# Turning the weights of GRU layers 1 to 3 in three places of two half-steps each, with the input weights and W in one PSUM bank

## The chip, the cores and the metric

The kernel runs on one core of a Trainium2 chip. The metric is the device time of one execution in microseconds (us). A run is a median of several executions. Of the engines, PE is TensorE (PEld its weight load), ACT is ScalarE, DVE is VectorE, POOL is GpSimd, and SP is SyncE, which here only issues DMAs.

## The reference, cut to what matters

```python
# layer 0: a gated graph network, 16 graphs of N = 1024 nodes, C = 128 features, L = 4 GRU layers
h = relu(layernorm(x))
for i in range(L):
    hw = h @ weight[i]
    m = adj.T @ hw                      # per graph
    gx = m @ w_ih[i].T + b_ih[i]        # 128 -> 3 x 128
    gh = h @ w_hh[i].T + b_hh[i]
    r, z = sigmoid(xr + hr), sigmoid(xz + hz)
    n = tanh(xn + r * hn)
    h = (1 - z) * n + z * h
x = x + h * mask
# layer 1: four graph convolutions with batch norm
h = relu(layernorm(x))
for i in range(4):
    h = batch_norm(relu(adj @ (h @ W[i]) + b[i]))
out = x + h
```

The change concerns only the weights of the GRU layers. The products with `weight[i]` and `w_ih[i]` follow each other without anything in between but the aggregation over nodes, so the kernel joins them: `weight[i] @ w_ih[i].T` is computed once per layer (`w_mT` in the code), and the aggregation works on `h` itself. For that the input weights, the hidden weights and `weight[i]` ("W" below, `w_g` in the code) have to be turned (transposed) once per layer, by PE.

## The kernel before

One program, `exact_path`, does the work; `general_path` (lines 20 to 356) is a fallback that is entered only when the inputs fail a test at run time. Features lie on the partitions, and a graph's 1024 nodes lie on the free axis in two halves of 512. The adjacency of a graph is held as eight rows of 128x1024, rounded to fp32r; the features are split into a high and a low part (`ghw`, two tiles), so the aggregation `aggregate_rows` (L521 to L531) is 32 matmuls of 128x512: eight rows, two parts, two halves. They add up in two PSUM banks, `pm`, which ACT copies to `m` (L944).

Two streams, `sa` and `sb`, each carry one graph at a time through its four layers. `half_step(one, two)` (L1035) aggregates one stream's layer while the gates of the other run: it splits `one`'s features (`split_step`, by eight turns `hw_g` at L498 in the first half-steps), does the gate products of `two` for its first and second half of nodes (`gate_step`, L955; six products each at L972, then sigmoid, tanh and sigmoid on ACT at L984, L990, L991, and the combination on DVE at L985, L986 and L997 to L999), then the first half of `one`'s aggregation, `agg_step(0)`, then whatever was passed as `halfway`, then `agg_step(1)`. What was passed as `gated` comes between the second gates and the aggregation. The kernel's clock counts half-steps and starts at 3; the stage before it, written out by hand from L1122, carries both graphs through their first aggregation. Half-step 3 is `half_step(sa, sb)`, with the aggregation of `sa` for its layer 1 and the gates of `sb` for its layer 0; half-step 4 is `half_step(sb, sa)`, and so on, two half-steps for each layer.

The order of instructions on an engine is the order of the code in the part under `manual_schedule(engines=every)`, which before ends with half-step 4. In the rest of the gated network it is the order of the code for PE, POOL and SP, and a scheduler orders ACT and DVE.

The weights come in natural layout by DMA on SP (`load_layer`, L457; layer 0 at the start, layers 1 to 3 later, then `w_g` for layers 1 to 3 at L1183). They are turned by `turn_layer` (L466): three turns of the hidden weights into one PSUM bank (L470) and an ACT copy of 384 columns (L471), three turns of the input weights into another (L474) and a copy (L477), one turn of W into a third (L479) and a copy of 128 columns (L481). `join_layer` (L484) multiplies the two turned matrices (L487) and copies the product to `w_mT` (L488). All these PSUM tiles come from `tmp`, a pool of two banks used in turn, which also serves `hw_g` and, in the part before half-step 5, `g_r` of the second half.

Layer 0 is turned and joined at the start, between L1129 and L1132. Layer 1 is turned at the half-way point of half-step 3 and joined at its end, layer 2 likewise in half-step 4, and layer 3 is turned and joined at once after that. The calls are:

```python
half_step(sa, sb, looks, lambda: turn_layer(prep, w_g, 1))
join_layer(1)
half_step(sb, sa, None, lambda: turn_layer(prep, w_g, 2))
join_layer(2)
turn_layer(prep, w_g, 3)
join_layer(3)
```

The hidden state of later half-steps leaves by DMA and comes back turned: DVE transposes blocks (L711), SP stores and reloads (L591, L598), ACT and DVE split it (L905, L906). SP also issues transposing loads of the adjacency (L610), from tiles that POOL casts (L609), and the rows of later graphs (L573), which POOL rounds (L578); a small POOL copy, `pace` (L1054), ties its queue to the gates. While the first graphs are read, DVE looks over each row (`first_look`, L604).

Of the kernel before, what the change touches and what calls it, by code (L numbers as in the profile page):

```python
# [8 lines left out]
F32 = mybir.dt.float32  # L9
# [7 lines left out]
P = 128  # L17
# [324 lines left out]
def exact_path(  # L342
# [21 lines left out]
    nc = tc.nc  # L364
    B, N, C = x.shape
    L = g_weight.shape[0]
    NB = N // P
# [11 lines left out]
    def acc(tag, name):  # L379
        return ps_m.tile([P, HALF], F32, tag=tag, name=name)  # L380

    def tmp(name):
        return ps_t.tile([P, HALF], F32, tag="tmp", name=name)
# [5 lines left out]
    def flat(name):  # L389
        return keep.tile([P, NB, C], F32, tag="x", name=name, bufs=4)  # L390
# [14 lines left out]
    ident = const.tile([P, P], F32, tag="ident", name="ident")  # L405
# [57 lines left out]

    turned = {}

    def turn_layer(prep, w_g, i):  # L466

        pt = tmp(f"pt_whh{i}")
        for g in range(3):
            nc.tensor.transpose(pt[:, g * P : (g + 1) * P], wns["hh", i][:, g, :], ident)  # L470
        nc.scalar.copy(w_hhT[:, i, :], pt[:, : 3 * P])  # L471
        pt = tmp(f"pt_wih{i}")
        for g in range(3):
            nc.tensor.transpose(pt[:, g * P : (g + 1) * P], wns["ih", i][:, g, :], ident)  # L474

        w_ihT = prep.tile([P, 3 * C], F32, tag="w_ihT", name=f"w_ihT{i}", bufs=1)
        nc.scalar.copy(w_ihT, pt[:, : 3 * P])  # L477
        pg = tmp(f"pt_g{i}")
        nc.tensor.transpose(pg[:, :P], w_g[:, i, :], ident)  # L479
        w_gT = prep.tile([P, P], F32, tag="w_gT", name=f"w_gT{i}", bufs=1)  # L480
        nc.scalar.copy(w_gT, pg[:, :P])  # L481
        turned[i] = w_gT, w_ihT

    def join_layer(i):  # L484
        w_gT, w_ihT = turned[i]
        pw = tmp(f"pt_wm{i}")
        nc.tensor.matmul(pw[:, : 3 * P], w_gT, w_ihT, start=True, stop=True)  # L487
        nc.scalar.copy(w_mT[:, i, :], pw[:, : 3 * P])  # L488
# [45 lines left out]
    with ExitStack() as st:  # L534
# [32 lines left out]
        def first_look(b, j, ts):  # L567
            for k, t in enumerate(ts):
                look(b, t, j, k)
# [42 lines left out]
        def transposes(batches):  # L612

            for b, rows in batches:
                adjT = turned_tile(f"adjT{b}")
                ahead = transpose_rows(b, rows[0], 0, adjT)
                for j in range(NB):
                    go = ahead
                    if j + 1 < NB:
                        ahead = transpose_rows(b, rows[j + 1], j + 1, adjT)  # L620
                    go()
                    yield j
                nc.gpsimd.dma_start(adjT_d[b].rearrange("k p n -> p k n"), adjT)
                yield NB
# [136 lines left out]
        def behind(*inss):  # L761

            es = ExitStack()
            for ins in () if written[0] else inss:
                es.enter_context(tc.issue_after(ins.ins))
            return es
# [264 lines left out]
        def due(place):  # L1031
            for go in agenda.pop((clock[0], place), ()):
                go()

        def half_step(one, two, gated=None, halfway=None):  # L1035

            feed.next_step()
            one.split = []
            if one.i == 0:
                two.fetch()  # L1040
            due("ins")
            if one is sb and one.i == 0 or written[0] and one is sa:
                feed.jobs = transposes([(s.b, s.rows) for s in (sa, sb)])
            if one.i > 0:
                one.split_step()
                two.fetch()
                feed.some(2)
            two.gate_step(0)
            two.half_away(0)
            two.first_four()  # L1050
            if feed.full or (clock[0], "mid") in agenda:

                pace = small.tile([P, 1], F32, tag="pace", name=f"pace{clock[0]}")
                nc.gpsimd.tensor_copy(pace, two.new[:, :1])  # L1054
                feed.store()
                due("mid")
            due("outs")
            one.split_back(0, two.last_act, two.mid_dve)
            one.split_back(1, two.last_act, two.mid_dve)
            if one.i > 0:  # L1060
                feed.some(1)
            two.gate_step(1, None, one.split)
            two.half_away(1)
            with behind(two.first_act):
                due("late")
            if one.i == 0:
                feed.some(1)
            two.last_four()
            if gated:
                gated()  # L1070
            if one.i == 0:
                with behind(two.last_m):
                    one.split_step()
            one.agg_step(0)
            if halfway:
                halfway()
            with behind(two.last_act, two.last_dve, *one.split):
                due("gap")
            feed.some(NB if written[0] and one is sa else 1)
            one.agg_step(1)  # L1080
            two.finish()
            clock[0] += 1

        sa, sb = Stream(0), Stream(1)
        every = {getattr(mybir.EngineType, e) for e in ("PE", "DVE", "Activation", "Pool", "SP")}
        with tc.tile_pool(name="prep", bufs=1) as prep, tc.manual_schedule(engines=every):


            pt = tmp("pt_idle")
# [14 lines left out]
            w_g = flat("w_g")[:, :L, :]  # L1104
# [21 lines left out]
            sa.sums(range(4, 5))  # L1126
            norm_invert(sa.norm, 0, BH)
            sa.centred(range(4))
            turn_layer(prep, w_g, 0)  # L1129
            sa.centred_high(0)  # L1130
            sa.sums(range(5, 7))
            join_layer(0)  # L1132
            pt = tmp("pt_idle1")
# [51 lines left out]
            sb.agg_rows(range(4))  # L1185
            turn(sb.y, "in1", h1)
            sb.hT = h1
            sb.agg_rows(range(4, NB))

            def looks():  # L1190
                for j in range(4, NB):
                    first_look(1, j, raw1[j])

            sa.plan(0)
            sb.plan(1)
            half_step(sa, sb, looks, lambda: turn_layer(prep, w_g, 1))
            join_layer(1)
            half_step(sb, sa, None, lambda: turn_layer(prep, w_g, 2))
            join_layer(2)
            turn_layer(prep, w_g, 3)  # L1200
            join_layer(3)
        with tc.manual_schedule(engines={getattr(mybir.EngineType, e) for e in ("PE", "Pool", "SP")}):
            written[0] = False
            for s in range(2, B // 2 * L):
                half_step(sa, sb)
                half_step(sb, sa)
            assert not agenda, sorted(agenda)
            sb.gate_step(0)
            sb.gate_step(1)
            with tc.issue_after(sb.last_act.ins):  # L1210
                sa.rest()
            sb.finish()
# [5 lines left out]
    pt = tmp("pt_flag")  # L1218
# [212 lines left out]
    pt = tmp("pt_idle_end")  # L1431
# [4 lines left out]
    for b in range(B):  # L1436
# [3 lines left out]
        for n0, n in pieces(b):  # L1440
# [5 lines left out]
            tag = turns[count % len(turns)]  # L1446
            count += 1
            pt = (tmp(f"pt_o{b}_{n0}") if tag == "tmp" else acc(tag, f"pt_o{b}_{n0}"))[:, :n]
# [8 lines left out]
@with_exitstack  # L1457
def kernel(ctx: ExitStack, tc: tile.TileContext, *args):
    nc = tc.nc
    flagp = ctx.enter_context(tc.tile_pool(name="flagp", bufs=1))  # L1460
    flag_i = flagp.tile([1, 1], I32, tag="flag", name="flag_i")
    exact_path(tc, flag_i, *args)
    inexact = nc.values_load(flag_i, min_val=0, max_val=1 << 24)  # L1463
    with tc.If(inexact > 0):
        general_path(tc, *args)
# [41 lines left out]
```

## Time and profile before

| what | value |
|---|---|
| median of three runs | 1796.03 us (1793.29 to 1797.85) |
| profiled execution, from first to last instruction (its span; no other time is given for it) | 1795.0 us |
| mean granted TensorE clock | 0.997 |
| PE busy in the span | 1763.4 us |
| DVE, ACT, POOL busy | 1258.8, 1107.2, 389.4 us |
| PE idle for ACT `ghw` (L905), whole span | 11.1 us, 7 times |
| turns of hidden weights, input weights, W (L470, L474, L479): first and last start | 6.7 to 82.6 us |
| products (L487): first and last start | 8.6 to 83.9 us |

A row of a timeline gives the start from the span's beginning, the busy time of the merged instructions, the engine, the source line, the operation, the tiles (written <- read), the shape and the count; brackets hold the engine's idle time ahead of the row and who ended it. PE is pipelined and a row's end is modelled: rows overlap, so the work of one step is better read from its start to the next one's start. An fp32 matmul shows as two rows (x2), an fp32r matmul and a 128-column turn as one. Line numbers are those of the kernel before; after the change most lines are one lower in the helpers and higher towards the end.

### The profile page before, as it was taken

To read this page: it belongs to the slowest core of one execution; us is meant where nothing else is said; L and a number is where in the kernel's file an instruction comes from. 1 tells how busy PE (TensorE), PEld (TensorE's weight loads), DVE (VectorE), ACT (ScalarE), POOL (GpSimd) and SP (SyncE) were. 2 spreads that over 40 slices of the span, in tenths; PEclk is the share of its full clock that TensorE was granted. 3 is DMA by queue.
4 is the path that set the end of the run, shared out by engine and by line. 5 is a ranking of instruction groups with operands and counts; after the bars stand their busy time and mean duration, and the time that the engine had idled before them with its cause. 6 is when DMAs were issued, how large, how long until landed. Compare 5 with 4: busy or idle time off the path is not lost. (4 is left out here: it accounts for less than half of the span.)

```text
span 1795.0 us, 22286 instructions
## 1 busy us (share of the span) xinstructions
PE 1763.4 (98%) x6742; PEld 1194.0 (67%) x6742; DVE 1258.8 (70%) x2308; ACT 1107.2 (62%) x1717; POOL 389.4 (22%) x417
## 2 busy tenths in 40 slices
PE   9999999999999999999999999999999999999997
PEld 6555565556565556556556555677778888888886
DVE  7567867867776776777786776676666666666665
ACT  5346456556556555755655655477777767768765
POOL 4213322332332331422342333110100000000011
PEclk9999999999999999999999999999999999999999
DMA  7448676776676766766767667778866566767667
GB/s 253 112 125 268 171 223 237 200 207 225 205 211 211 236 191 193 263 197 168 263 185 209 241 194 209 268 277 299 284 223 244 209 244 215 246 223 240 241 220 263
DMA packets 363968, 399.11 MB, mean 222 GB/s; under 512 B 159820, under 2 KB 240496, under 8 KB 363840
## 3 DMA queue, kind: packets, MB, share of 16 engines
q1 hardware_dynamic: 343088, 322.54, 57.1%
q0 software_dynamic: 20224, 74.80, 11.5%
q8 instruction: 55, 0.90, 0.2%
q14 instruction: 73, 0.60, 0.1%
q10 hardware_dynamic: 528, 0.26, 0.0%
HBM read 266.95 MB, written 96.99 MB: 203 GB/s over the span
## 5 line engine op out<-in xcount | busy, mean ns | idle before, releaser
L525 PE MATMUL pm<-row,ghw 128*128 128x512 f32 x2048 | 505.6, 403 | 11.8 <-ACT ghw L905 11.1
L525 PEld LDWEIGHTS pm<-row,ghw 128*128 128x128 f32 x2048 | 384.3, 189 | 124.5 <-issue 26.5
L525 PE MATMUL pc_m<-wide,chw 128*128 128x512 f32 x1024 | 246.1, 396 | 0.0
L609 POOL CAST half<-row 128x1024 bf16<-128x1024 f32 x128 | 148.8, 1171 | 327.2 <-DMA adjT<-half 312.5
L525 PEld LDWEIGHTS pc_m<-wide,chw 128*128 128x128 f32 x1024 | 190.5, 188 | 42.3 <-issue 4.3
L991 ACT ACTIVATE z<-g_z,brz 128x512 f32<-128x512 f32 x128 | 87.5, 684 | 171.3 <-PE g_z L972 171.2
L525 PE MATMUL pc_g_r<-wide,chw 128*128 128x512 f32 x464 | 187.0, 403 | 0.3 <-ACT chw L502 0.3
L578 POOL CAST row<-stage 128x1024 fp32r<-128x1024 f32 x112 | 131.5, 1181 | 243.6 <-DMA stage<-in_adj_dram 221.1
L525 PE MATMUL pc_g_z<-wide,chw 128*128 128x512 f32 x464 | 181.0, 390 | 0.0
L985 DVE SCALAR_TENSOR_TENSOR r<-g_hn,vecs,r 128x512 f32<-128x512 f32 x128 | 95.0, 742 | 118.3 <-ACT r L984 76.6
L1237 DVE CAST wide<-block 128x1024 fp32r<-128x1024 bf16 x160 | 109.8, 692 | 73.2 <-PE pc_m L525 46.2
L1237 DVE CAST wide<-packed 128x1024 fp32r<-128x1024 bf16 x160 | 110.2, 691 | 72.1 <-PE pc_g_z L525 53.9
L944 ACT COPY m<-pm 128x512 f32<-128x512 f32 x128 | 68.5, 586 | 147.9 <-PE pm L525 147.9
L990 ACT ACTIVATE r<-r,vecs 128x512 f32<-128x512 f32 x128 | 91.8, 717 | 104.0 <-DVE r L986 104.0
L997 DVE TENSOR_TENSOR h<-h,r 128x512 f32<-128x512 f32 x96 | 81.8, 852 | 101.6 <-ACT r L990 101.6
L1235 ACT CAST wide<-packed 128x1024 fp32r<-128x1024 bf16 x96 | 100.6, 1048 | 59.1 <-PE pc_m L525 28.3
L972 PE MATMUL g_r<-m,w_mT 128*128 128x512 f32 x256 | 131.5, 595 | 2.8 <-ACT m L944 2.3
L1235 ACT CAST wide<-block 128x1024 fp32r<-128x1024 bf16 x96 | 100.6, 1049 | 52.3 <-PE pc_g_z L525 27.7
L972 PE MATMUL g_xn<-m,w_mT 128*128 128x512 f32 x256 | 130.7, 592 | 0.0
L972 PE MATMUL g_z<-m,w_mT 128*128 128x512 f32 x256 | 130.7, 592 | 0.0
L998 DVE TENSOR_TENSOR h<-h,z 128x512 f32<-128x512 f32 x128 | 118.7, 931 | 4.8 <-ACT z L991 1.9
L1285 DVE BATCH_NORM_STATS2 stats<-feat 128x6 f32<-128x512 f32 x128 | 84.1, 686 | 47.0 <-ACT feat L1284 45.9
(187 smaller groups left out, 2804.3 us busy)
## 6 DMA issues: line engine op xcount, KB each, us to landing
block<-adjT_d SPq DMA_DIRECT2D x256, 256.0 KB, 4.7
packed<-adjT_d SPq DMA_DIRECT2D x256, 256.0 KB, 5.5
stage<-in_adj_dram SPq DMA_DIRECT2D x120, 512.0 KB, 4.8
adjT_d<-adjT POOLq DMA_DIRECT2D x16, 2048.0 KB, 8.3
cross_h<-t_h SPq DMA_DIRECT2D x90, 256.0 KB, 3.2
n_h<-cross_h SPq DMA_DIRECT2D x360, 64.0 KB, 2.0
xmid_d<-x POOLq DMA_DIRECT2D x16, 512.0 KB, 5.4
y<-ymid_d POOLq DMA_DIRECT2D x16, 512.0 KB, 5.9
```

The source lines that it names most:

```text
L525: nc.tensor.matmul(pm[hf], hw[s][:, j * P : (j + 1) * P], rows[j][:, hf * HALF : (hf + 1) * HALF], start=(j == 0 and s == 0), stop=(j == N ...
L578: nc.gpsimd.tensor_copy(t, stage[j % 4])
L609: nc.gpsimd.tensor_copy(t, row.bitcast(F32))
L972: nc.tensor.matmul(po, wT[:, i, g * C : (g + 1) * C], rhs, start=start, stop=stop)
L985: nc.vector.scalar_tensor_tensor(r, phn, b_hn(i), r, ALU.add, ALU.mult)
L990: nc.scalar.activation(r, r, AF.Tanh, bias=b_in(i))
L991: self.last_act = nc.scalar.activation(z, pz, AF.Sigmoid, bias=brz[:, 3 * i + 1 : 3 * i + 2])
L997: nc.vector.tensor_sub(ho, hin, r)
L998: nc.vector.tensor_mul(ho, ho, z)
L1235: nc.scalar.copy(r, t)
L1237: nc.vector.tensor_copy(r, t)
L1285: nc.vector.bn_stats(stats[:, b * NH + hf, :], dst)
```

## The change

`turn_layer` is cut in two. `turn_hh(i)` turns and copies the hidden weights. `turn_ih(prep, w_g, i)` turns the input weights and W into the four quarters of one bank, and empties it by one copy of 512 columns into one tile, `w_both`, of which the product takes its two operands. The pool `prep` stays open longer.

Of layers 1 to 3, the hidden weights are turned at the half-way point of the half-step ahead (layer 1: between the sixth and the seventh row of `sb`'s first aggregation), the input weights and W after the gates of the layer's own half-step, and the product is made at its half-way point, followed there by the next layer's hidden weights. Layer 3 moves from the end of half-step 4 into half-step 5, which stands in the part that a scheduler orders for ACT and DVE. For layer 0 both functions are called where `turn_layer` was.

```diff
-    def turn_layer(prep, w_g, i):
+    def turn_hh(i):
         pt = tmp(f"pt_whh{i}")
         for g in range(3):
             nc.tensor.transpose(pt[:, g * P : (g + 1) * P], wns["hh", i][:, g, :], ident)
         nc.scalar.copy(w_hhT[:, i, :], pt[:, : 3 * P])
+
+    def turn_ih(prep, w_g, i):
         pt = tmp(f"pt_wih{i}")
         for g in range(3):
             nc.tensor.transpose(pt[:, g * P : (g + 1) * P], wns["ih", i][:, g, :], ident)
-        w_ihT = prep.tile([P, 3 * C], F32, tag="w_ihT", name=f"w_ihT{i}", bufs=1)
-        nc.scalar.copy(w_ihT, pt[:, : 3 * P])
-        pg = tmp(f"pt_g{i}")
-        nc.tensor.transpose(pg[:, :P], w_g[:, i, :], ident)
-        w_gT = prep.tile([P, P], F32, tag="w_gT", name=f"w_gT{i}", bufs=1)
-        nc.scalar.copy(w_gT, pg[:, :P])
-        turned[i] = w_gT, w_ihT
+        nc.tensor.transpose(pt[:, 3 * P :], w_g[:, i, :], ident)
+        both = prep.tile([P, 4 * C], F32, tag="w_both", name=f"w_both{i}", bufs=1)
+        nc.scalar.copy(both, pt)
+        turned[i] = both[:, 3 * C :], both[:, : 3 * C]
...
-            turn_layer(prep, w_g, 0)
+            turn_hh(0)
+            turn_ih(prep, w_g, 0)
...
-            sb.agg_rows(range(4, NB))
+            sb.agg_rows(range(4, 6))
+            turn_hh(1)
+            sb.agg_rows(range(6, NB))
             def looks():
+                turn_ih(prep, w_g, 1)
                 for j in range(4, NB):
                     first_look(1, j, raw1[j])
+            def ahead(i):
+                join_layer(i)
+                if i + 1 < L:
+                    turn_hh(i + 1)
             sa.plan(0)
             sb.plan(1)
-            half_step(sa, sb, looks, lambda: turn_layer(prep, w_g, 1))
-            join_layer(1)
-            half_step(sb, sa, None, lambda: turn_layer(prep, w_g, 2))
-            join_layer(2)
-            turn_layer(prep, w_g, 3)
-            join_layer(3)
+            half_step(sa, sb, looks, lambda: ahead(1))
+            half_step(sb, sa, lambda: turn_ih(prep, w_g, 2), lambda: ahead(2))
         with tc.manual_schedule(engines={getattr(mybir.EngineType, e) for e in ("PE", "Pool", "SP")}):
             written[0] = False
-            for s in range(2, B // 2 * L):
+            half_step(sa, sb, lambda: turn_ih(prep, w_g, 3), lambda: ahead(3))
+            half_step(sb, sa)
+            for s in range(3, B // 2 * L):
```

More of the change, by code (lines that the diff above doesn't have):

```diff
@@ L1085, in exact_path @@
         every = {getattr(mybir.EngineType, e) for e in ("PE", "DVE", "Activation", "Pool", "SP")}
-        with tc.tile_pool(name="prep", bufs=1) as prep, tc.manual_schedule(engines=every):
+        prep = st.enter_context(tc.tile_pool(name="prep", bufs=1))
+        with tc.manual_schedule(engines=every):
             pt = tmp("pt_idle")
```

## The prediction

> **What bounds the kernel now.** I read the head of the page first, then the waits of TensorE (PE), then the stretch that the edit touches, row by row. From the page (busy time with its share, then the PE and clock rows of the forty slices):
>
> ```profile
> span 1795.0 us, 22286 instructions
> PE 1763.4 (98%) x6742; PEld 1194.0 (67%) x6742; DVE 1258.8 (70%) x2308; ACT 1107.2 (62%) x1717; POOL 389.4 (22%) x417
> ...
> PE   9999999999999999999999999999999999999997
> ...
> PEclk9999999999999999999999999999999999999999
> ```
>
> PE is busy in every slice at full clock. A busy PE is not yet a PE at its peak, but the 31.6 us it sat idle are the only time that can be won without removing matmuls. Where they lie in the first 110 us is told by PE's waits in that window (waiter, then releaser: total us, times, longest):
>
> ```profile
> PE pt_wm L487 <- ACT w_gT L481: 1.0, 2, 0.6
> PE pt_g L479 <- ACT w_hhT L471: 0.7, 3, 0.2
> ...
> PE pt_wih L474 <- ACT w_mT L488: 0.3, 1, 0.3
> PE hw_g L498 <- ACT w_mT L488: 0.2, 1, 0.2
> PE g_r L972 <- DVE ghw L503: 0.2, 1, 0.2
> ```
>
> Four of these five are the weight turning: PE waits for a ScalarE (ACT) copy of what it has just turned. The timeline of PE shows the largest such place, the end of half-step 4 (start us, busy us, instruction; in brackets the idle time ahead of it):
>
> ```profile
> 75.80 0.49 PE L470 MATMUL pt_whh<-ident,wn_hh 128*128 128x128 f32 x3
> 76.13 0.49 PE L474 MATMUL pt_wih<-ident,wn_ih 128*128 128x128 f32 x3
> 76.86 0.33 PE L479 MATMUL pt_g<-ident,w_g 128*128 128x128 f32 x1 [0.24 <-ACT w_hhT L471]
> 76.94 3.91 PE L525 MATMUL pm<-row,ghw 128*128 128x512 f32 x16
> 80.69 0.81 PE L487 MATMUL pt_wm<-w_ihT,w_gT 128*128 128x384 f32 x2
> 81.33 0.49 PE L470 MATMUL pt_whh<-ident,wn_hh 128*128 128x128 f32 x3
> 82.17 0.55 PE L474 MATMUL pt_wih<-ident,wn_ih 128*128 128x128 f32 x3 [0.35 <-ACT w_mT L488]
> 82.56 0.33 PE L479 MATMUL pt_g<-ident,w_g 128*128 128x128 f32 x1
> 83.51 0.91 PE L487 MATMUL pt_wm<-w_ihT,w_gT 128*128 128x384 f32 x2 [0.62 <-ACT w_gT L481]
> 84.26 1.39 PE L498 MATMUL hw_g<-ident,h 128*128 128x128 f32 x8
> 85.48 1.02 PE L972 MATMUL g_r<-h,w_hhT 128*128 128x512 f32 x2
> ```
>
> From 80.69 to 85.48 no aggregation matmul stands between a turn and the step that needs its copy. Rows overlap, since ends are modelled, so I count from start to start below.
>
> **What the Trainium skill says.** "PSUM — Partial Sum Buffer", section on bank collisions: guard PSUM by bank and quadrant, not by address. So a turn into a bank waits for the copy out of it; the trace agrees (L479 waits 0.24 us for the copy of L471, its bank's last reader). "Perfetto Trace Analysis", Matmuls: independent groups should rotate through banks so that a copy overlaps the next group. Here two banks carry three turns and a product, and the 82.17 row shows the rotation running dry. "ScalarE: Activation LUTs", What ACT_TABLE_LOAD costs: an activation with immediate operands takes 186 ns plus 0.833 ns per element, and successive ones overlap by about 93 ns. The trace has 478 ns for 384 columns and 266 ns for 128, somewhat less than the 506 and 293 of that rule, with starts about 0.1 us before the previous end. I use the trace's durations.
>
> **The change part by part.** Unit prices, start to start: three turns 0.32 us (54.99 to 55.31), so 0.107 each; the product L487 0.64 (59.88 to 60.52); eight unhindered hw_g turns 0.88 (39.67 to 40.55); one gate product 0.86; sixteen aggregation matmuls 3.75 (56.13 to 59.88). The number of turns and products is the same before and after, so what can change is stall.
>
> *Stalls removed.* Half-step 3: 55.31 to 56.05 is 0.74, less 0.32 of work, 0.42 of stall; hw_g 60.52 to 61.36 is 0.84, less 0.43, 0.41. Half-step 4: 76.13 to 76.86 stalls 0.41; 81.33 to 82.17 stalls 0.52; 82.56 to 83.51 stalls 0.95 - 0.11 = 0.84; 83.51 to 84.26 stalls 0.11; hw_g, 84.26 to 85.48, is 1.22 against 0.88, 0.34. Sum 0.83 + 2.22 = 3.05 us. Check by whole steps: from the last gate product to the next gate, half-steps 3 and 4 take 11.38 (50.47 to 61.85) and 14.18 (71.30 to 85.48); half-step 5, without turns, takes 8.15 (94.93 to 103.08), with hw_g 9.03. The excess is 2.35 + 5.15 = 7.50; 21 turns and 3 products are 2.25 + 1.92 = 4.17; 3.33 is stall. So 3.05 can be named and 0.28 can't.
>
> *Hidden weights of layer 1, moved ahead.* turn_hh(1) puts 0.32 us of PE work at about 38 us, between rows 4-5 and 6-7. Soon after, g_r waits for VectorE (DVE): 44.84 to 46.08 is 1.24 against 0.86, a stall of 0.38, and DVE is busy with its looks without a gap from 38.3 to 46.5, independent of PE. So the 0.32 moves into a stall: a further gain of 0.32. Without that cover it is 0. Its copy falls into ACT's 2.77 us wait ahead of the m copies at 39.64. Its data were asked for at 26.30 and land in about 3.3 us.
>
> *Input weights and W, after the second gate.* Four turns (0.43) now stand ahead of the first aggregation row, into one bank, emptied by one 512-column copy. The nearest row is the m copy of 128x512, 586 ns. That copy is behind tanh and the z sigmoid on ACT's queue. In half-step 3 z runs 53.20 to 53.87, so the copy ends at about 54.4. PE turns at 51.33 to 51.76, aggregates 3.75, and asks for it at 55.5: cover 1.1 us. In half-steps 4 and 5 the same sum gives 76.4 against 74.2 and 100.0 against 97.2: cover 2.2 and 2.8. If the cover failed, each microsecond of lateness would be a microsecond of PE. w_g was asked for at 43.53 and lands in 3.7 to 5.1, at the latest 48.6, against 51.3.
>
> *Product and next hidden weights at half way.* The two tmp banks have been emptied by then: product and turn go through without waiting, their copies (about 0.5 each) have the second 3.75 us of aggregation as cover, and hw_g at its end finds both banks free.
>
> *Layer 3 a half-step later.* Layer 3 is now joined in the middle of half-step 5; its first gate is three half-steps on, in half-step 8. So nothing waits for it.
>
> *Layer 0.* One copy (0.59) in place of two (0.49 and 0.27, overlapping): L487 could start at about 8.54 instead of 8.63. Four aggregation matmuls later PE waits for POOL's row anyway (10.02 to 11.46 is 1.44, of which 0.94 work). Worth 0.
>
> *Queues.* DVE, POOL and SP keep their order. The two built programs differ in one wait that matters: the load of wn_hh2 now waits for turn_hh(1) on PE, whose buffer it evidently takes, where it waited for DVE until 41.34. PE is there at 38.4, so SP isn't held; the next load waits for DVE as before.
>
> *New borders.* Turns stand between aggregation rows in four new places. In 30.64 to 40.55, 9.91, I find 8.15 + 0.88 for step and hw_g and 0.88 for eight turns in the middle, 0.11 each: borders cost nothing there. Not shown is a border with a semaphore on PE's queue; I bound it between 0 and 0.15 us each and take 0. It can't gain, as it adds a wait.
>
> *Sum.* 3.05 + 0.32 = 3.4 us, with ends 3.65 (the unnamed 0.28 goes too) and 2.5 (borders 0.6, turn_hh(1) uncovered 0.3). Nothing later should give it back: the transpose loads on SP end at 86.97, and SP then waits 6.8 us for DVE before its next store at 93.82; after that, stores, reloads and stage loads are all paced by the gates, and PE's largest later wait, 11.1 us in all for ghw of L905, starts from the gates as well. Span 1795.0 - 3.4 = 1791.6. The page gives no other time of its execution; the median of the runs shown, 1796.0, is 1.0 above its span, so I forecast 1792.6.
>
> **Rivals.**
> - *The gain is swallowed.* PE starts half-step 5 earlier, but a chain with its own clock (transpose loads, POOL casts, staging of the next batch) doesn't, and a later wait absorbs the lead. For: POOL waits 312.5 us in all for transpose loads. Against: the 6.8 us of slack just named, and no PE wait for POOL rows after 13 us. Leaves 0 to 1 us: 1795.5.
> - *More than the stalls.* The waits for L905 differ between batches (1.28 at five places, 1.93 and 2.80 at two). They hang on how DMA traffic falls. Another phase could bring the two to 1.28, another 2.2 us: 1790.4.
> - *Slower: the reload falls behind the transposes.* With PE ahead by 3.4, the SP queue could have a transpose load in front of the hidden-state stores L591 at each half-batch. Seven L905 waits going from 1.3 to the 2.8 seen once cost 10 us, less 3.4: 1802.6. It decides once the lead exceeds the 6.8 us of slack, or if loads are stretched by as much. Only the 2.80 speaks for it.
> - *It doesn't do what it says:* w_both's copy is late in half-step 3. It would take a lateness of over 1.1 us; gain then 2.4 or less, inside the range.
>
> **How the numbers follow.** Forecast 0.62, its own range 1791.4 to 1794.5; swallowed 0.16; more 0.15; slower 0.07. Three runs of the kernel before span 4.6 us, so a median may be off by some 1.5 either way. Low end 1789.0 (the larger gain less that), high end 1797.0 (swallowed plus that). About 0.3%, 5.4 us, is what a measurement of this kernel can tell from no change. Faster by that needs the larger gain with noise on its side: 0.15. Slower by that is only the third rival: 0.06. Same: 0.79.
>
> **What would show it.** Right: no PE idle at the product or the turns between 50 and 100 us; half-step 3 from 11.4 to about 10.4, half-step 4 from 14.2 to about 10.4, half-step 5 from 8.15 to about 9.2; the first gate of half-step 6, at 103.08, about 3.4 earlier, and that lead kept at 1700. Wrong: a wait of the product for w_both; a lead of 3.4 at 100 us that is gone by 350; L905 waits above 1.3 in number; or g_r at about 46 us later than before.

## The result, and the profile after

Sixteen runs of each kernel, taken in turns, give a median of 1792.83 us (1790.73 to 1796.87) for the changed kernel against 1796.66 us (1793.29 to 1799.67) for the one before. The ratio is 0.9981 with a 95% interval of 0.9974 to 0.9989: 2.0 to 4.7 us faster, and less than the 0.3% that was called no change.

The head of the changed kernel's page:

```profile
span 1789.3 us, 22282 instructions
PE 1759.7 (98%) x6742; PEld 1191.5 (67%) x6742; DVE 1264.2 (71%) x2308; ACT 1107.8 (62%) x1713; POOL 388.9 (22%) x417
```

The number of PE instructions is unchanged, and ACT has lost the four W copies. The span is 5.7 us below the other profile's 1795.0, more than the medians differ, so a single pair of spans must not be read as the gain. It is read from the half-steps. First PE's waits in the first 110 us of the changed kernel:

```profile
PE pt_idle L1093 <- POOL ident masks.py:199: 2.4, 1, 2.4
PE pt_wm L486 <- ACT w_both L480: 0.7, 1, 0.7
PE g_z L971 <- ACT z L990: 0.6, 1, 0.6
PE g_r L971 <- DVE ghw L502: 0.3, 1, 0.3
```

Of the four kinds of waits for weights that stood in the list of before, one is left, and its one case is layer 0's product at 7.6 us. The timeline of PE through half-step 4, the stretch that was shown of before:

```profile
69.63 1.02 PE L971 MATMUL g_z<-m,w_mT 128*128 128x512 f32 x2
70.49 0.49 PE L477 MATMUL pt_wih<-ident,wn_ih 128*128 128x128 f32 x3
70.82 0.27 PE L478 MATMUL pt_wih<-ident,w_g 128*128 128x128 f32 x1
70.85 3.94 PE L524 MATMUL pm<-row,ghw 128*128 128x512 f32 x16
74.62 0.81 PE L486 MATMUL pt_wm<-w_both 128*128 128x384 f32 x2
75.27 0.49 PE L470 MATMUL pt_whh<-ident,wn_hh 128*128 128x128 f32 x3
75.51 3.92 PE L524 MATMUL pm<-row,ghw 128*128 128x512 f32 x16
79.27 1.03 PE L497 MATMUL hw_g<-ident,h 128*128 128x128 f32 x8
80.14 1.02 PE L971 MATMUL g_r<-h,w_hhT 128*128 128x512 f32 x2
```

No row has a bracket: PE goes from turns to aggregation to product to turns without a wait. From the last gate product (69.63) to the next gate (80.14) it takes 10.51 us, where it took 14.19. ACT in the same stretch shows why:

```profile
71.43 0.67 ACT L990 ACTIVATE z<-g_z,brz 128x512 f32<-128x512 f32 x1
72.00 0.57 ACT L480 COPY w_both<-pt_wih 128x512 f32<-128x512 f32 x1
75.46 0.48 ACT L487 COPY w_mT<-pt_wm 128x384 f32<-128x384 f32 x1 [2.89 <-PE pt_wm L486]
75.84 0.48 ACT L471 COPY w_hhT<-pt_whh 128x384 f32<-128x384 f32 x1
79.24 1.08 ACT L943 COPY m<-pm 128x512 f32<-128x512 f32 x2 [2.91 <-PE pm L524]
```

The w_both copy ends at 72.57 and its reader, the product, starts at 74.62, 2.05 us later; the next two copies end 2.9 us ahead of the m copies. The first half of the aggregation covers the w_both copy, the second half the other two.

The three half-steps, each from its last gate product to the next gate, in all kernels whose profile bears on them:

| kernel | 3 | 4 | 5 | sum | against before |
|---|---|---|---|---|---|
| before (twice the same) | 11.38 | 14.19 | 8.15 | 33.72 | |
| changed (second profile 10.46, 10.48, 9.31) | 10.49 | 10.51 | 9.31 | 30.31 | -3.41 |
| merge alone | 10.95 | 13.81 | 8.15 | 32.91 | -0.81 |
| places alone | 10.48 | 10.51 | 9.31 | 30.30 | -3.42 |
| layer 3 at once | 10.48 | 13.20 | 8.13 | 31.81 | -1.91 |
| product without cover | 14.78 | 11.73 | 10.39 | 36.90 | +3.18 |
| product without cover, wait filled | 13.21 | 11.60 | 10.36 | 35.17 | +1.45 |
| no turns | 9.00 | 9.00 | 8.13 | 26.13 | -7.59 |

The stretch ahead of half-step 3, in which layer 1's hidden weights are now turned, is not in these sums; it is looked at below.

### The profile page after: what moved, and what is told of

It is laid out like the page before. It is cut to its first block, busy times and chain, and to the rows that moved or that the text cites. A ratio compares the mean times of both kernels' runs of the same rounds, so it can differ in the third digit from the quotient of the medians.

```text
span 1789.3 us, 22282 instructions
## 1 busy us (share of the span) xinstructions
PE 1759.7 (98%) x6742; PEld 1191.5 (67%) x6742; DVE 1264.2 (71%) x2308; ACT 1107.8 (62%) x1713; POOL 388.9 (22%) x417
## 5 line engine op out<-in xcount | busy, mean ns | idle before, releaser
L524 PE MATMUL pm<-row,ghw 128*128 128x512 f32 x2048 | 503.8, 402 | 11.2 <-ACT ghw L904 10.9
```

What stands on the lines that cost most here:

```text
L524: nc.tensor.matmul(pm[hf], hw[s][:, j * P : (j + 1) * P], rows[j][:, hf * HALF : (hf + 1) * HALF], start=(j == 0 and s == 0), stop=(j == N ...
```

## The experiments

**The merge alone.** The kernel before, with one bank and one copy for input weights and W:

```diff
-        w_ihT = prep.tile([P, 3 * C], F32, tag="w_ihT", name=f"w_ihT{i}", bufs=1)
-        nc.scalar.copy(w_ihT, pt[:, : 3 * P])
-        pg = tmp(f"pt_g{i}")
-        nc.tensor.transpose(pg[:, :P], w_g[:, i, :], ident)
-        w_gT = prep.tile([P, P], F32, tag="w_gT", name=f"w_gT{i}", bufs=1)
-        nc.scalar.copy(w_gT, pg[:, :P])
-        turned[i] = w_gT, w_ihT
+        nc.tensor.transpose(pt[:, 3 * P :], w_g[:, i, :], ident)
+        both = prep.tile([P, 4 * C], F32, tag="w_both", name=f"w_both{i}", bufs=1)
+        nc.scalar.copy(both, pt)
+        turned[i] = both[:, 3 * C :], both[:, : 3 * C]
```

> The kernel before, with only the merge: W is turned into the fourth quarter of the input weights' bank and one copy of 512 columns empties it; all places stay. Theory (stalls counted row by row): only the two stalls of 0.42 and 0.41 us of the W turn behind the w_hhT copy go, at half-steps 3 and 4. The row of products and turns at the end of half-step 4 keeps its 2.2 us. Half-step 3 about 10.9 us, half-step 4 about 13.7; 0.8 us faster than before, not to be told from it by time. Rival (the merge with its shorter chain of copies is what wins): most of the 3.4 us, half-step 4 near 11.

Measured: 0.81 us in the half-steps; ratio 0.9998 (0.9989 to 1.0006). The end of half-step 4 on PE in this kernel:

```profile
79.82 0.49 PE L470 MATMUL pt_whh<-ident,wn_hh 128*128 128x128 f32 x3
80.66 0.55 PE L474 MATMUL pt_wih<-ident,wn_ih 128*128 128x128 f32 x3 [0.35 <-ACT w_mT L485]
81.04 0.27 PE L476 MATMUL pt_wih<-ident,w_g 128*128 128x128 f32 x1
82.04 0.91 PE L484 MATMUL pt_wm<-w_both 128*128 128x384 f32 x2 [0.73 <-ACT w_both L478]
82.79 1.39 PE L495 MATMUL hw_g<-ident,h 128*128 128x128 f32 x8
84.02 1.02 PE L969 MATMUL g_r<-h,w_hhT 128*128 128x512 f32 x2
```

The row of turn, copy, product, copy is still there: one larger copy is waited for as long as two small ones. The rival falls.

**The places alone.** The changed kernel with the diff above turned round inside `turn_ih`.

> The changed kernel without the merge: the new places, but W in a bank of its own and two copies (384 and 128 columns) as before. Theory (the places win, the copies are covered wherever they are): half-steps 3, 4 and 5 take 10.5, 10.5 and 9.3 us as in the changed kernel, no wait of PE for a copy of weights; 3.4 us faster than before. Rival (two banks don't suffice for three turned matrices, the merge is needed): a wait of the W turn or of the product for a copy comes back, 0.4 us or more in each of three half-steps, so about 2 us faster than before at most.

Measured: the half-steps of the changed kernel to 0.02 us; ratio 0.9985 (0.9978 to 0.9991). In half-step 3 ACT does the two copies one after the other:

```profile
53.01 0.67 ACT L993 ACTIVATE z<-g_z,brz 128x512 f32<-128x512 f32 x1
53.58 0.47 ACT L479 COPY w_ihT<-pt_wih 128x384 f32<-128x384 f32 x1
53.93 0.28 ACT L483 COPY w_gT<-pt_g 128x128 f32<-128x128 f32 x1
56.08 0.48 ACT L490 COPY w_mT<-pt_wm 128x384 f32<-128x384 f32 x1 [1.87 <-PE pt_wm L489]
```

They end at 54.21, and the product that reads them starts at 55.24, behind PE's first half aggregation. With the new places the merge adds nothing; it is worth its 0.8 us only in the old ones. Two banks suffice for three turned matrices here, as soon as half an aggregation stands between turns and product.

**Layer 3 at once.**

```diff
             half_step(sb, sa, lambda: turn_ih(prep, w_g, 2), lambda: ahead(2))
+            turn_ih(prep, w_g, 3)
+            join_layer(3)
...
-            half_step(sa, sb, lambda: turn_ih(prep, w_g, 3), lambda: ahead(3))
+            half_step(sa, sb)
```

> The changed kernel, but the input weights and W of layer 3 are turned and joined at the end of half-step 4 instead of in half-step 5 (its hidden weights stay at the half-way point of half-step 4). Theory: the product waits for the 512-column copy behind the turns, about 0.65 us, and the second hw_g group for the product's copy, about 0.4; the work of 1.07 us moves from half-step 5 to 4. Half-step 4 about 12.6, half-step 5 about 8.15 us; about 1.1 us of the 3.4 is lost. Rival (layer 3's move is worth nothing, its stalls came from the third turn group alone): half-step 4 about 11.6.

Measured: 1.50 us of the gain lost, not 1.1; ratio 0.9992 (0.9983 to 1.0000). ACT tells the difference:

```profile
79.38 1.07 ACT L943 COPY m<-pm 128x512 f32<-128x512 f32 x2 [2.91 <-PE pm L524]
80.34 0.60 ACT L480 COPY w_both<-pt_wih 128x512 f32<-128x512 f32 x1
81.95 0.48 ACT L487 COPY w_mT<-pt_wm 128x384 f32<-128x384 f32 x1 [1.00 <-PE pt_wm L486]
```

The last of the turns starts on PE at 79.74, but their copy starts only at 80.34: the two m copies, free only at the end of the aggregation, stand ahead of it on ACT's queue. I had left that queue out. So moving layer 3's input weights, W and product brings 1.5 of the 3.4 us.

**The product without its cover.**

```diff
+            def turn_join(i):
+                turn_ih(prep, w_g, i)
+                join_layer(i)
...
             def looks():
-                turn_ih(prep, w_g, 1)
+                turn_join(1)
...
             def ahead(i):
-                join_layer(i)
                 if i + 1 < L:
                     turn_hh(i + 1)
...
-            half_step(sb, sa, lambda: turn_ih(prep, w_g, 2), lambda: ahead(2))
+            half_step(sb, sa, lambda: turn_join(2), lambda: ahead(2))
...
-            half_step(sa, sb, lambda: turn_ih(prep, w_g, 3), lambda: ahead(3))
+            half_step(sa, sb, lambda: turn_join(3), lambda: ahead(3))
```

> The changed kernel, but each product of layers 1 to 3 stands right behind the turns of its operands, ahead of the aggregation, instead of half-way. Theory (the half aggregation is the cover of the w_both copy, which queues on ScalarE behind tanh and sigmoid): PE waits from the end of the turns to the end of the copy, 2.6, 1.65 and 1.6 us in half-steps 3, 4 and 5, 5.9 us in all, so 5.9 us slower than the changed kernel and about 2.5 slower than before. Rival (PE's idle time here is taken up by later waits): PE waits as said but the end moves by less than 2 us.

Measured: 6.59 us more than the changed kernel in the half-steps, 4.29, 1.22 and 1.08, where 2.6, 1.65 and 1.6 were expected; ratio 1.0022 (1.0012 to 1.0031), slower than before. The end moved, so the rival falls. Half-steps 4 and 5 lost about half a microsecond less each than expected, because there the w_both copy ends sooner after the last gate product than in the changed kernel, 2.39 and 2.28 us against 2.94 and 2.90; the reason is given under *Input weights and W* below. Half-step 3 has 1.7 us too much. PE there, and then the engines' busy time in two stretches (PE, PEld, DVE, ACT and POOL, then granted clock, DMA share and GB/s):

```profile
51.17 0.27 PE L478 MATMUL pt_wih<-ident,w_g 128*128 128x128 f32 x1
53.90 1.02 PE L486 MATMUL pt_wm<-w_both 128*128 128x384 f32 x2 [2.46 <-ACT w_both L480]
54.36 5.71 PE L524 MATMUL pm<-row,ghw 128*128 128x512 f32 x16
59.90 0.49 PE L470 MATMUL pt_whh<-ident,wn_hh 128*128 128x128 f32 x3
```

```profile
54.00:58.00 4.00, 4.00 (x10) 3.02 (x11) 3.97 (x5) 0.48 (x1) 0.00 (x0) 0.57 0.00 0
58.00:60.00 2.00, 2.00 (x10) 1.59 (x10) 1.55 (x2) 0.00 (x0) 0.00 (x0) 1.00 0.00 0
```

Sixteen aggregation matmuls span 5.54 us from start to start where 3.8 to 4.1 is usual. The granted clock in the four microseconds is 0.57; the clock records have it at 0.5 from 54.57 to 57.99, 3.42 us, and there a matmul follows the last after 427 ns instead of about 230, so those inside the stretch took nearly twice their time and all sixteen together 1.4 times. That came 0.7 us after PE had stood idle 2.46 us.

**The same, with the wait filled.** Turns of the identity that nobody reads, 20, 8 and 8, between turns and product:

```diff
-            def turn_join(i):
+            def turn_join(i, n=8):
                 turn_ih(prep, w_g, i)
+                pt = tmp(f"pt_fill{i}")
+                for k in range(n):
+                    nc.tensor.transpose(pt[:, k % 4 * P : (k % 4 + 1) * P], ident, ident)
                 join_layer(i)
...
-                turn_join(1)
+                turn_join(1, 20)
```

> The run with the product right behind its turns, and 20, 8 and 8 turns of the identity, that nobody reads, between the two in half-steps 3, 4 and 5. There half-step 3 took 14.78 us, 1.7 more than the wait for the copy explains, and behind PE's idle 2.46 us sixteen aggregation matmuls took twice their time at half the granted clock. Theory (the idle stretch itself brings the clock down): with PE kept busy the clock stays whole, half-step 3 takes 13.1 us though the product comes no sooner; half-step 4 and 5 stay at 11.7 and 10.4. Rival (the clock fell by chance, or the looks of VectorE slow the matmuls): 14.8 again.

```profile
51.19 2.35 PE L1197 MATMUL pt_fill<-ident 128*128 128x128 f32 x20
53.82 0.91 PE L486 MATMUL pt_wm<-w_both 128*128 128x384 f32 x2 [0.28 <-ACT w_both L480]
54.27 4.14 PE L524 MATMUL pm<-row,ghw 128*128 128x512 f32 x16
58.25 0.49 PE L470 MATMUL pt_whh<-ident,wn_hh 128*128 128x128 f32 x3
```

Half-step 3 takes 13.21 us. The product comes as late as without filling, 2.74 us behind the last weight turn after 2.73, and the aggregation behind it takes 3.98 us instead of 5.54. DVE's looks start in the same place behind the product (54.88, and 54.96 without filling), so they aren't what slowed the matmuls. So the idle stretch itself cost another 1.6 us through the clock. It is one profile of each, and the last section adds what all profiles say of it.

**More work on PE at 80 us.** 64 turns of the identity ahead of half-step 5:

```diff
             half_step(sb, sa, lambda: turn_ih(prep, w_g, 2), lambda: ahead(2))
+            pt = tmp("pt_extra")
+            for k in range(64):
+                nc.tensor.transpose(pt[:, k % 4 * P : (k % 4 + 1) * P], ident, ident)
```

> The changed kernel with 64 more turns of the identity on PE at the end of half-step 4 (work added that nobody reads). Theory (PE sets the pace from there to the end, so a delay at 80 us arrives whole): 64 times 0.107 us, 6.85 us slower than the changed kernel, about 3.4 slower than before; the lag stays at 6.9 at 300 and 1700 us. Rival (later chains with a clock of their own absorb it): lag falls, under 3 us at the end.

```profile
80.12 7.15 PE L1209 MATMUL pt_extra<-ident 128*128 128x128 f32 x64
87.11 1.04 PE L497 MATMUL hw_g<-ident,h 128*128 128x128 f32 x8
87.98 1.02 PE L971 MATMUL g_r<-h,w_hhT 128*128 128x512 f32 x2
```

They take 6.99 us. Counted from the last gate product of layer 0's first graph, PE's first wait for reloaded state, at about 200 us, comes 6.9 us later than in the changed kernel, the second, at about 340, 6.9, and the seventh, at about 1060, 7.1. The final turns of the kernel come at 1739.6 us, with one stretch of half clock on the way, against 1730.9 in the changed kernel, which had none. Less 1.7 for that stretch, half of its 3.42, the lag is 7.0: nothing absorbs it. (This last figure is rough: corrected in the same way, the two profiles of before differ by 2.5.) The ratio is 1.0034 (1.0024 to 1.0045), 0.53% above the changed kernel's where 0.38% was expected, a little more than the trace shows; the two intervals are just wide enough.

**No turns.** The turns, copies and products of layers 1 to 3 are left out, and those layers' gates read layer 0's turned weights:

```diff
-                nc.tensor.matmul(po, wT[:, i, g * C : (g + 1) * C], rhs, start=start, stop=stop)
+                nc.tensor.matmul(po, wT[:, 0, g * C : (g + 1) * C], rhs, start=start, stop=stop)
...
-            sb.agg_rows(range(4, 6))
-            turn_hh(1)
-            sb.agg_rows(range(6, NB))
+            sb.agg_rows(range(4, NB))
...
-                turn_ih(prep, w_g, 1)
...
-            half_step(sa, sb, looks, lambda: ahead(1))
-            half_step(sb, sa, lambda: turn_ih(prep, w_g, 2), lambda: ahead(2))
+            half_step(sa, sb, looks)
+            half_step(sb, sa)
...
-            half_step(sa, sb, lambda: turn_ih(prep, w_g, 3), lambda: ahead(3))
+            half_step(sa, sb)
```

> The changed kernel with no turns, copies and products of the weights of layers 1 to 3 at all; left out is their computation, and layers 1 to 3 use layer 0's turned weights. Theory (no stall is left in the changed kernel, only work: 21 turns and 3 products, 4.2 us, of which the first three turns lie in a wait): half-steps 3, 4 and 5 take 9.0, 9.0 and 8.15 us, 4.0 us faster than the changed kernel and 7.3 faster than before. Rival (borders between turns and aggregation still cost): more than 5 us faster than the changed kernel.

Measured: 4.18 us less than the changed kernel in the half-steps; ratio 0.9961 (0.9948 to 0.9973), 3.6 us below the changed kernel's ratio. The work that fell there is 18 turns and 3 products, 1.93 + 1.92 = 3.85 us. The changed kernel has 0.33 us left there that isn't work, about 0.11 in each half-step, and no wait.

**The hidden weights of layer 1, later or with more beside them.** Late: turned in half-step 3, right ahead of `turn_ih(prep, w_g, 1)`. More: 12 turns of the identity behind them.

```diff
-            turn_hh(1)
             sb.agg_rows(range(6, NB))
...
             def looks():
+                turn_hh(1)
                 turn_ih(prep, w_g, 1)
```

> The changed kernel, but the hidden weights of layer 1 are turned in half-step 3, right ahead of its input weights, and not between rows 5 and 6 of the aggregation before. Theory (at 38 us the three turns lie in PE's wait for VectorE at 46 us): half-step 3 takes 10.8 us instead of 10.5, and nothing is won ahead of it: from the last gate product of layer 0's first graph to the second gate of half-step 3, 15.5 us as in all runs so far (15.4 to 15.9), so the whole is 0.3 us slower. Rival (the turns weren't covered): half-step 3 10.8 and that stretch 15.1 or less.

```diff
             turn_hh(1)
+            pt = tmp("pt_extra")
+            for k in range(12):
+                nc.tensor.transpose(pt[:, k % 4 * P : (k % 4 + 1) * P], ident, ident)
             sb.agg_rows(range(6, NB))
```

> The changed kernel with 12 more turns of the identity behind the hidden weights of layer 1, at about 38 us: 1.28 us of PE work there in addition to 0.32. Theory (the wait for VectorE covers about 0.4 us, and 0.32 is taken): the stretch from the last gate product of layer 0's first graph to the second gate of half-step 3 grows from 15.5 to 16.6 or 16.7 us. Rival (VectorE sets that point with much more room, or it follows PE): 15.5 to 15.9, or 16.8 and over.

The stretch meant is that from the last gate product of layer 0's first graph to the second gate of half-step 3. Late: half-step 3 took 10.81 us, the stretch ahead of it 15.44. More: the stretch took 16.74. With no PE work at that place the stretch is thus 15.4 to 15.6 in five profiles; with 0.32 us it is 15.4 to 15.5 in six and 15.8 and 15.9 in two; with 1.60 us it is 16.74. Less these 1.60 PE alone would take 15.14, so the wait for DVE covers about 0.3 us, just what was put there. The 15.9 is the first profile of the changed kernel: there PE still waits 0.3 us for DVE, behind the turns.

**Both kernels once more,** for one more profile each.

> The kernel before once more, for one more profile. The profiled span of before was 1795.0 and that of the changed kernel 1789.3, 5.7 us apart where the medians differ by 3.8; 0.7 us of it lies ahead of the first turn of weights (6.73 against 6.01), where the two programs are the same. Theory (the start and the waits for reloads vary from one execution to the next): the first turn, the aggregation's start and the long ghw waits shift by up to about 1 us from the first profile, half-steps 3, 4 and 5 repeat within 0.1 us at 11.4, 14.2 and 8.15. Rival (the start belongs to the program): 6.73 again within 0.1.

> The changed kernel once more, for one more profile. Theory: half-steps 3, 4 and 5 repeat within 0.1 us at 10.5, 10.5 and 9.3; the first turn of weights shifts from 6.01 as it likes; span within 3 us of 1791.6. Rival (the change itself makes the start earlier): 6.01 again within 0.1.

Spans 1801.4 and 1794.8 us; the second missed 1791.6 by 3.2, just outside what was expected. Each of these two executions had 10.2 us at half clock, where the first profiles had 3.4 (before) and none (changed), so spans tell of the clock as much as of the change. The half-steps repeated within 0.03 us. The first turn of weights came at 6.60 us (6.73 in the first profile of before) and at 6.19 (6.01 in that of the changed kernel). Twenty turns of the identity stand ahead of it on PE, and follow each other after 0.21 us until the clock records rise to full and after 0.11 from then on, so the first turn depends on when the rise comes: at 7.05 and 6.45 us in the two profiles of before, 5.26 and 5.62 in the two of the changed kernel, but from 5.29 to 8.28 in the others, whatever the edit. Nine of these have the changed kernel's start, and their first turn comes between 6.03 and 6.73. So the 0.7 us at the start isn't the change's.

**Filled waits, an attempt at a faster kernel.** In the profiles the clock fell for 3.42 us (twice for 6.8) near the last wait for reloaded state, of 2.8 us or more, in 9 of the 13 profiles in which these waits aren't filled, and in 5 of 78 near the six earlier ones of 1.3 to 2.2 us.

```diff
+            if clock[0] > 3 and clock[0] % 8 == 3:
+                pt = tmp(f"pt_fill{clock[0]}")
+                for k in range(20 if clock[0] == 59 else 8):
+                    nc.tensor.transpose(pt[:, k % 4 * P : (k % 4 + 1) * P], ident, ident)
             one.agg_step(0)
```

> The changed kernel with turns of the identity, that nobody reads, put on PE where it waits for the reloaded hidden state ahead of an aggregation: 8 turns (0.86 us) in each of the six waits of 1.3 us, 20 (2.1 us) in the last one of 2.8. In the profiles so far the granted clock falls to half for 3.42 us behind such a wait in some executions (none, one or up to three times in each), and PE's matmuls take twice as long there. Theory (the idle stretch lets the clock fall, and that makes the scatter between executions): no stretch at half clock between the start and the end of the profile, the runs closer together than 4 us, the median about 2 us below the changed kernel's, ratio to before about 0.997. Rival (the clock falls for another reason, or the extra turns delay the aggregation): stretches at half clock stay, or the aggregation starts later, and the median is that of the changed kernel or above.

The profile had no stretch at half clock, but neither had three of the 13 without fillers. The median is 1795.06 us, ratio 0.9988 (0.9978 to 0.9998), and the runs scatter by 5.4 us. That doesn't beat the changed kernel. In the profile PE still waits for the reloaded state behind the fillers at all seven places, 6.5 us in all, and the seven aggregations start 18.1 us in all after the last gate products ahead of them, against 14.7 to 16.7 in the other 13 profiles: the state itself came back later. Whether the fillers did that is not shown. That the clock makes the scatter between executions is not shown either; what does stays open.

## Why the prediction was right, step by step

- *Sum.* 3.4 us were forecast; the half-steps gave 3.41, the medians 3.8, the ratio 3.4. The forecast was 1792.6, the median 1792.83. That it is this near is luck: the median of before turned out 0.6 above the one I started from, and the sixteen runs of the changed kernel lie 6.1 us apart. The 1.0 us that I added to the span has no meaning of its own either, since each execution takes 1.7 to 1.9 us more than its own span.
- *Stalls removed, 3.05.* Right. The waits are gone, and the merge alone took back 0.81 of the 0.83 us booked for the two W turns.
- *The unnamed 0.28.* I kept it as a possible extra gain, and it didn't come. With the run without turns as the base, 0.37 us of the kernel before are neither work nor named stalls (7.59 less 4.17 less 3.05), and 0.33 of the changed kernel. That this is the price of borders between turns and aggregation is an inference; no run separates it.
- *New borders, 0.* Mis-sized, if the 0.33 is theirs: about 0.1 us in each half-step with turns, so that half-steps 3 to 5 took 10.5, 10.5 and 9.3, each some 0.1 above forecast. In the sum it cancelled, because the kernel before had about as much.
- *Hidden weights of layer 1.* Right, and with nothing to spare: cover 0.3, work 0.32.
- *Input weights and W.* Cover of 1.1, 2.2 and 2.8 us was forecast; it was 1.1, 2.05 and 2.1. In half-step 5 ACT's copy ended at 92.49 and the product stood at 94.58. What I missed there is POOL. A cast of 1.04 us on POOL starts at 86.92, one of DVE's gate rows (L998) at 87.00, and that row takes 1.50 us where it took 0.69 in the kernel before, with no cast beside it; tanh, the z sigmoid and the copy follow later. In half-step 4 two such rows take 1.54 and 1.41 us beside casts. Over the whole profile of the changed kernel the 212 rows of this kind with no cast beside them have a median of 0.69 us, and the 125 that overlap one by more than 0.3 us a median of 1.41. In the run without cover the casts fell on them less (1.15 and 1.34 us in half-step 4, 0.69 throughout in half-step 5), which fits the smaller loss there. That run puts a price on the cover, 6.6 us in all, 1.6 of it through the clock.
- *Layer 0, worth 0.* The product still waits for its copy, 0.68 us. No run tells a gain from the start's scatter.
- *Queues.* Right. SP issued the wn_hh2 load at 37.1 us behind turn_hh(1), and the next load waited for DVE until 40.6, as before.
- *Rivals.* Swallowed: no, the extra turns show that a shift at 80 us reaches the end whole. Slower by transpose loads: the waits for ghw sum to 10.9 us after 11.1. More than the stalls: the 2.8 stayed 2.8.
- *A sign that failed:* the first gate of half-step 6 was to come 3.4 us earlier and came 4.2 earlier, and the final turns 5.7. Beside the change the 4.2 holds 1.3 us of start, less 0.5 by which the stretch ahead of half-step 3 was longer, and the 5.7 also, at 205 us in the profile of before alone, a stretch of half clock. I should have named half-step lengths alone. I had also read full clock in every slice off the page, where a slice is 45 us and its digit 9 means 90% or more: that hides a stretch of 3.4 us.

## What to carry to other kernels

When PE waits for a copy of its own result, find a place where the copy has other PE work in front of its reader; that alone was worth 3.4 us here, and sharing a bank to save a copy added nothing to it. Count from start to start against a step of the same kind without the edited work, and look at what is queued ahead of the copy: the m copies cost the run with layer 3 at once 0.4 us that a count of copies alone missed. Where runs scatter by 6 us, a gain of 3 is best read from step lengths, which repeated within 0.03 us.

## What the runs showed of the hardware that was not expected

A single idle stretch of PE of 2.46 us was followed by 3.42 us at half the granted clock, which cost another 1.6 us; with filler work in that stretch it didn't happen (one profile of each). The Trainium skill ("TensorE: Matmul & The Clock Gate", Why this matters for your kernels) advises against idle gaps of more than about 3 us; here one of 2.46 was enough, while in four profiles of 13 a last wait for reloaded state of 2.8 to 2.95 us was not.

The 14 profiles say what decides here, besides the length. In each of them the clock changes only at whole multiples of 3.413 us after its first rise. I divided each profile into windows of that length from the rise on, 7277 in all, and took the share of each window in which no PE row runs (the ends of rows are modelled, so the shares are rough). All 10 windows that are idle for more than 0.56 are followed by a window at half clock; of the 11 between 0.45 and 0.56 five are; of those under 0.45 none is, except that in two profiles the half clock lasted for a second window. The 2.46 us lay inside one window, from 51.16 to 54.57, which was idle for 0.72. In the four profiles without a half-clock stretch at the last wait, that wait was split over two windows, neither idle for more than 0.54. So what counted was how much of one window stood idle, and the same wait can cost a clock stretch in one execution and none in the next. With fillers in these waits no window of the profile was idle for more than 0.43, and none ran at half clock; it didn't make the kernel faster.

DVE rows on 128x512 elements that took 0.69 us alone took about 1.4 with a POOL cast beside them, and so moved a copy on ACT that has nothing to do with POOL.
